# A four-layer graph network on one core: second norm as a factor on ScalarE, edge digits behind the norms, far blocks spread out, count writes issued from ScalarE

## The chip, the cores and the metric

The kernel runs on one core of one Trainium2 chip. The metric is the device time of a whole execution in microseconds (us). The kernel before took 5277.65 us as the median of three runs (5276.34 to 5281.7).

## The reference, cut to what matters

Four layers of a graph network act on 3125 nodes with 256 features and 103,125 edges (50,000 random pairs in both directions, and a loop on every node). Each layer adds a graph attention and a second mixing branch to `x`, and then a feed-forward network. The change touches only what comes first in layer 0:

```python
edge_index = jnp.stack([src, dst])
xn = _layernorm(x, axis=-1)             # (x - mean) / sqrt(var + 1e-5), no weights
x = x + _L0_gnn_ref(xn, edge_index, ...)[...] + _L0_mix_ref(xn[None], ...)[0]
```

`_L0_gnn_ref` is an attention over the edges: each node takes a softmax-weighted sum over its incoming edges. `_L0_mix_ref` takes `xn` as it is for a linear attention over all nodes (a context from keys and values), and it normalizes `xn` a second time, with `ln_g` and `ln_b`, for a gate network (256 to 64, gelu, 64 to 256, sigmoid).

## The kernel before, in words

The nodes lie as 25 tiles of 125 rows (`TP` = 125, `NT` = 25). Work on tiles goes by `GROUPS`: four groups of four tiles, then three of three. The kernel turns the edge list into a dense matrix of counts (how many edges go from source s to destination d), stored in DRAM, and computes graph attention as dense products with these counts.

**Stage A, `begin` (L1592) and `prepare` (L1473).** `run` (L2855) loads x in four pieces (4, 4, 8 and 9 tiles), each by `part_dma` (L571), which issues two DMAs (112 rows and 13 rows), on SP's and ScalarE's queues in turn. `prepare` is a generator. Its first part loads the row table `heads_i` and the destinations, counts by five passes over the table (L1495) where each block of five nodes begins in the sorted edge list, and gathers five edge segments by GpSimd (L1501). `begin` then goes through the groups: `layernorm` (L610: `moments` with L622 and L623, `normed` with a Sqrt on ScalarE L631, a reciprocal L632 and one scaling per tile L634), `transposed` (L286: TensorE transposes L293, one copy to `xT` on ScalarE L301 and one on VectorE L299), and the checks: for every group the matmuls into `p_ends`. For the first four groups it also adds the tiles to the context of keys and values (`context_tile`, L1630: two f32 matmuls per tile with an Exp and a Copy on ScalarE, a memset on GpSimd, two matmuls into `p_ctx`). When `prepare` is sent the fourth group, it first calls `edges()` (L1505): some twenty operations on VectorE that turn the gathered segments into digits (L1509 to L1521), write them to DRAM as `seg_d`, and count the edges found (L1527 to L1545). After the last group the checks are reduced to one number `ok`, on which the kernel branches.

**Stage B, `counts` (L1688).** It reads `seg_d` back, transposes it to digits by edge (L1713, evicted by ScalarE L1715), and goes through 625 groups of five destination nodes in 63 steps of ten groups. In a step VectorE builds two one-hot tiles, `oh_lo` (L1734) and `oh_key` (L1737), from a pool of two buffers. TensorE multiplies them into `p_cnt` (L1750; four PSUM buffers, three used in a step), and ScalarE evicts `p_cnt` as bytes into `stage` (L1752; two buffers). Five steps make a block of 250 destinations. In the five blocks named in `FAR` ScalarE also evicts it as bf16 into `far` (L1755; one buffer). `BLOCKS` gives the order: 8, 0, 9, 1, 10, 2, 11, 3, 12, 4, 5, 6, 7. After a block, SP's queue writes `stage` to `count_d` (L1759, 781 KB) and, for a far block, `far` to `far_d` (L1762, 1562 KB).

Between the steps `counts` advances a second generator, `mix0_pieces` (L1769), at a fixed rate of 93 pieces over 63 steps: `node_pieces` (L1835: projections of the nodes, whose small results go to DRAM by SP's queue, L1856 and L1860), `fold_pieces` (L1651: the other nine tiles of the context), one large addition on GpSimd (L1786), and then by groups the gate network, which begins with `layernorm(xn, xn, group)`, the second norm, in place on VectorE.

**Stage C, `dense_pairs` (L1919).** Its order is written out by hand for all engines. SP's queue loads a row of factors (`q_head`, L1974) and tiles of counts (`a`, L1912; `a_far`, L2019). VectorE multiplies them into `pt` (L1986), and TensorE sums (L2000). For the far destinations ScalarE and GpSimd prepare `pt_far`.

**Order.** Outside of stage C the order of the instructions on each engine and queue is set by the framework's planner. It takes the operations by their place in the program as priority, but moves one ahead of another when its own estimate says that the other isn't ready. Each engine then runs its instructions strictly in that order, DMA issues included: a DMA that can't be issued holds all that stands behind it on the same engine.

Of the kernel before, what the change touches and what calls it, by code (L numbers as in the profile page):

```python
# [10 lines left out]
F32 = mybir.dt.float32  # L11
# [38 lines left out]
NEAR0 = (0, 8)  # L50
FAR0 = (16, 9)
FAR = [8, 9, 10, 11, 12]
BLOCKS = [8, 0, 9, 1, 10, 2, 11, 3, 12, 4, 5, 6, 7]
BEFORE = 4
GROUPS = [(0, 4), (4, 4), (8, 4), (12, 4), (16, 3), (19, 3), (22, 3)]

# [1407 lines left out]
class Dense(Net):  # L1464
# [8 lines left out]
    def prepare(self, pool, xT):  # L1473
# [6 lines left out]
        with ExitStack() as s:  # L1480
# [66 lines left out]

            group = yield
            while group:
                if group == GROUPS[3]:  # L1550
                    found = edges()
                for t in range(group[0], sum(group)):
                    self.mm(p_ends[:, t, :], [(xT[:, k, t * TP:(t + 1) * TP], gw[:, k, C:]) for k in range(KC)])
                group = yield
# [37 lines left out]
    def begin(self, pool, x, xn, xT):  # L1592

        nc, tc = self.nc, self.tc
        self.ctx_d = self.dram.tile([P, KC * (P + 1)], F32, name="ctx_d")
        with ExitStack() as s:
            c = s.enter_context(tc.tile_pool(name="c0", bufs=1))
            w = s.enter_context(tc.tile_pool(name="c0w", bufs=2))  # L1600
            pst = s.enter_context(tc.tile_pool(name="c0t", bufs=2, space=PSUM))
            ps = s.enter_context(tc.tile_pool(name="c0p", bufs=2, space=PSUM))
            ps1 = s.enter_context(tc.tile_pool(name="c0c", bufs=1, space=PSUM))
            wkv = self.keys_weight(c)
            checks = self.prepare(pool, xT)
            next(checks)
            p_ctx = ps1.tile([P, KC, P + 1], F32, name="p_ctx")
            self.context_bank(w, p_ctx, True)
            self.layernorm(xn, x, GROUPS[0])
            for i, (t0, nt) in enumerate(GROUPS):  # L1610
                self.transposed(pst, xT, xn, groups=[GROUPS[i]])
                if i + 1 < len(GROUPS):
                    self.layernorm(xn, x, GROUPS[i + 1])
                checks.send(GROUPS[i])
                if i < BEFORE:
                    for t in range(t0, t0 + nt):
                        self.context_tile(w, ps, p_ctx, xT, wkv, t)
            self.context_bank(w, p_ctx, False)
            part = c.tile([P, KC, P + 1], F32, name="ctx_part")
            nc.scalar.activation(part, p_ctx, AF.Copy)  # L1620
            nc.sync.dma_start(self.ctx_d, part.rearrange("p m f -> p (m f)"))
            next(checks, None)
# [65 lines left out]
    def counts(self, pieces, later):  # L1688


        nc, tc = self.nc, self.tc
        self.count_d = self.dram.tile([NS, P, N], U8, name="count_d")
        self.far_d = self.dram.tile([NS, P, FAR0[1] * TP], BF16, name="far_d")
        B = 10
        with ExitStack() as s:
            c = s.enter_context(tc.tile_pool(name="cnt", bufs=1))
            w = s.enter_context(tc.tile_pool(name="cntw", bufs=2))
            wo = s.enter_context(tc.tile_pool(name="cnto", bufs=1))
            wf = s.enter_context(tc.tile_pool(name="cntf", bufs=1))
            work = pieces(c, wo)  # L1700
            by_edge = []
            ps = s.enter_context(tc.tile_pool(name="cntp", bufs=4, space=PSUM))
            seg = []
            for i in range(2):
                seg.append(w.tile([P, P, 2 * B], BF16, name="oh_lo").rearrange("p a b -> p (a b)").bitcast(F32)[:TP].rearrange("p (g s) -> p g s", s=SEG))
                self.part_dma(nc.scalar if i else nc.sync, seg[i], self.seg_d[i])
            for i, name in enumerate(("lo_t", "key_t")):
                R = 2 if i else 1
                t = c.tile([P, NG, 2, R], BF16, name=name)
                for b in range(GN):  # L1710
                    p = ps.tile([P, 4, KEYS], F32, name="p_cnt")
                    for j in range(2):
                        nc.tensor.transpose(p[:, j, :TP], seg[i][:, b, j * P:(j + 1) * P], self.ident[:TP, :TP])  # L1713
                    for r in range(R):
                        nc.scalar.activation(t[:, b * TP:(b + 1) * TP, :, r], p[:, :2, :TP].rearrange("p i g -> p g i"), AF.Copy)  # L1715
                by_edge.append(t)
            later()
            lo_t, key_t = by_edge
            is_lo = c.tile([P, P, 2 * B], BF16, name="is_lo")
            nc.vector.tensor_copy(is_lo, self.iota[:, :, None].to_broadcast([P, P, 2 * B]))  # L1720
            KP = KEYS + KEYS % 2
            is_key = c.tile([P, KP], BF16, name="is_key")
            nc.vector.tensor_scalar(is_key, self.iota[:, :KP], -127.0, None, op0=OP.add)
            is_pair = is_key.rearrange("p (k r) -> p k r", r=2)
            stage = None
            done, steps = 0, -(-NG // B)
            order = [g0 for k in BLOCKS for g0 in range(k * 50, min(k * 50 + 50, NG), B)]
            for step, g0 in enumerate(order):
                n = min(B, NG - g0)
                m = 2 * n  # L1730
                lo = lo_t[:, g0:g0 + n].rearrange("p g i r -> p (g i r)")
                key = key_t[:, g0:g0 + n].rearrange("p g i r -> p (g i) r")
                oh_lo = w.tile([P, P, 2 * B], BF16, name="oh_lo")
                nc.vector.tensor_tensor(oh_lo[:, :, :m], lo[:, None, :].to_broadcast([P, P, m]), is_lo[:, :, :m], OP.is_equal)  # L1734

                oh_key = w.tile([P, 2 * B, KP], BF16, name="oh_key")
                nc.vector.tensor_tensor(oh_key[:, :m].rearrange("p m (k r) -> p m k r", r=2),  # L1737
                                        key[:, :, None, :].to_broadcast([P, m, KP // 2, 2]),
                                        is_pair[:, None].to_broadcast([P, m, KP // 2, 2]), OP.is_equal)
                at = g0 * GN % 250  # L1740
                if at == 0:
                    stage = w.tile([P, NS, 250], U8, name="stage")
                    far = wf.tile([P, NS, 250], BF16, name="far") if g0 * GN // 250 in FAR else None
                for u in range(0, n, 4):
                    m = min(4, n - u)
                    p = ps.tile([P, 4, KEYS], F32, name="p_cnt")
                    for g in range(m):
                        for i in range(2):
                            j = 2 * (u + g) + i
                            nc.tensor.matmul(p[:, g, :], oh_lo[:, :, j], oh_key[:, j, :KEYS], start=(i == 0), stop=(i == 1))  # L1750
                    o = stage[:, :, at + u * GN:at + (u + m) * GN]
                    nc.scalar.activation(o.rearrange("p t (g d) -> p t g d", d=GN),  # L1752
                                         p[:, :m, :].rearrange("p g (t d) -> p t g d", d=GN), AF.Copy)
                    if far is not None:
                        nc.scalar.activation(far[:, :, at + u * GN:at + (u + m) * GN].rearrange("p t (g d) -> p t g d", d=GN),  # L1755
                                             p[:, :m, :].rearrange("p g (t d) -> p t g d", d=GN), AF.Copy)
                if at + n * GN == 250 or g0 + n == NG:
                    d0, nd = g0 * GN - at, at + n * GN
                    nc.sync.dma_start(self.count_d[:, :, d0:d0 + nd].rearrange("t p d -> p t d"), stage[:, :, :nd])  # L1759
                    if far is not None:  # L1760
                        f0 = FAR.index(d0 // 250) * 250
                        nc.sync.dma_start(self.far_d[:, :, f0:f0 + nd].rearrange("t p d -> p t d"), far[:, :, :nd])  # L1762
                while done < (step + 1) * PIECES0 // steps:
                    next(work, None)
                    done += 1
            for _ in work:
                pass

    def mix0_pieces(self, x, xn, xT, nodes, c, w):  # L1769
# [3 lines left out]
        with ExitStack() as s:  # L1773
# [13 lines left out]
            for t0, nt in GROUPS:  # L1787
                n = nt * TP
                cs = slice(t0 * TP, t0 * TP + n)
                xnn = xn[:, t0:t0 + nt, :]  # L1790
                self.layernorm(xn, xn, (t0, nt))
                yield
                xnnT = w.tile([P, KC, 512], F32, name="xnnT")
                for k in range(KC):
# [1060 lines left out]
    def run(self, x_in, out):  # L2855
# [5 lines left out]
        xn = self.xn_all[:TP]  # L2861
        xT = pool.tile([P, KC, N], F32, name="xT")
        x_v = x_in.rearrange("(t p) c -> p t c", p=TP)
        for i, (t0, nt) in enumerate(((0, 4), (4, 4), (8, 8), (16, 9))):
            self.part_dma(nc.scalar if i % 2 else nc.sync, x[:, t0:t0 + nt, :], x_v[:, t0:t0 + nt, :])
        out_v = out.rearrange("(t p) c -> p t c", p=TP)
        self.begin(pool, x, xn, xT)
# [191 lines left out]
```

## Time and profile before

| what | us |
|---|---|
| median of three runs | 5277.65 |
| profiled execution, its own time | 5526.72 |
| its span, first to last instruction | 5524.8 |
| stage A, to the last write of `ok` | 0 to about 104.6 |
| stage B, from the branch to the last addition to x | 105.4 to 379.2 |
| first VectorE product of stage C | 390.49 |
| last matmul of stage C's end pieces | about 1050 |

Over the whole span TensorE is busy for 4815.9 us, VectorE for 3534.0, ScalarE for 1574.9 and GpSimd for 1522.3. In the first 1035 us TensorE is busy for 918.35 us, VectorE for 854.22, ScalarE for 724.98 and GpSimd for 509.47.

How to read it: a line of the order of time gives the start, the length, the engine, the line of the kernel, the operation with what it writes and reads, how many in a row, and in brackets how long the engine had been idle and what ended that. A letter q after an engine (SPq, ACTq) marks a DMA issue on its queue; its length is the time of the issue, not of the transfer. The profiled execution is longer than the runs without profiling, so that differences in it are compared with its own time.

### The profile page before, as it was taken

The numbers are of one execution on the slowest core, as the hardware profiler recorded it, in microseconds if no ns is written. First come the engines' busy times: TensorE is split into PE (matmuls) and PEld (weight loads), VectorE is DVE, ScalarE is ACT, GpSimd is POOL, SyncE is SP. The second block draws the span as 40 slices with busy tenths as digits, with TensorE's granted clock in tenths as the row PEclk, the third lists the DMA queues.
The fourth block names the chain that finished last, engine by engine and source line by source line (L and its number), as shares of the span: only waits on it lengthen the run. The fifth ranks groups of instructions, "written<-read, shape, count | busy, mean of one in ns | idle before, by whom it ended". The sixth has DMA issues, their size and how long they took to land. (4 is left out here: it accounts for less than half of the span.)

```text
span 5524.8 us, 68126 instructions
## 1 busy us (share of the span) xinstructions
PE 4815.9 (87%) x24840; PEld 2883.0 (52%) x24840; DVE 3534.0 (64%) x5869; ACT 1574.9 (29%) x2503; POOL 1522.3 (28%) x1398
## 2 busy tenths in 40 slices
PE   6889989788888999899998999999967767687768
PEld 4554434477454333686453434556644545454457
DVE  6978888655656998454458997323266666556643
ACT  3668868311421001102330001333311012222221
POOL 1118858244000000000100000000066655555533
PEclk8899999789999999999999999999977888888879
DMA  3875535412100111110001112000154455445535
GB/s 88 89 90 159 160 107 162 134 55 77 49 1 27 34 41 30 43 36 12 14 1 42 39 29 67 14 0 1 37 145 135 137 149 150 135 129 153 143 118 175
DMA packets 353191, 443.06 MB, mean 80 GB/s; under 512 B 144846, under 2 KB 273229, under 8 KB 352278
## 3 DMA queue, kind: packets, MB, share of 16 engines
q1 hardware_dynamic: 264514, 219.66, 16.5%
q0 software_dynamic: 53744, 171.34, 10.8%
q10 hardware_dynamic: 34593, 47.63, 2.8%
q8 instruction: 202, 3.31, 0.2%
q14 instruction: 138, 1.13, 0.1%
HBM read 384.86 MB, written 56.78 MB: 80 GB/s over the span
## 5 line engine op out<-in xcount | busy, mean ns | idle before, releaser
L2289 POOL DMA_INDIRECT z_edge<-tab,src_i x806 | 774.6, 961 | 533.2 <-issue 217.3
L1905 DVE SCALAR_TENSOR_TENSOR pt<-q_head,bar,a 128x750 f32<-128x750 f32 (+2 forms) x800 | 776.3, 1025 | 62.5 <-PE acc L2135 53.8
L2130 PE MATMUL acc<-pt,zs 128*64 128x375 f32 (+2 forms) x3200 | 603.6, 501 | 24.0 <-DVE pt L1905 23.8
L2357 PE MATMUL p_acc<-z_edge,oh 128*125 128x264 f32 x2044 | 555.9, 434 | 41.3 <-DVE z_edge L2348 27.4
L2031 POOL TENSOR_TENSOR pt_far<-pt_far,a_far 128x1125 f32<-128x1125 f32 (+1 forms) x200 | 474.9, 2375 | 280.1 <-DMA a<-count_d 143.6
L2357 PEld LDWEIGHTS p_acc<-z_edge,oh 128*125 128x125 f32 x2044 | 434.4, 217 | 141.8 <-DVE z_edge L2348 29.8
L1986 DVE SCALAR_TENSOR_TENSOR pt<-q_here,bar,a 128x1000 f32<-128x1000 f32 (+1 forms) x384 | 456.1, 1250 | 37.2 <-DMA a<-count_d 15.9
L2130 PEld LDWEIGHTS acc<-pt,zs 128*64 128x64 f32 (+1 forms) x3200 | 247.0, 136 | 357.4 <-issue 221.0
L2000 PE MATMUL p_n<-pt,zs 128*64 128x500 f32 (+1 forms) x1600 | 405.9, 598 | 27.8 <-DVE pt L1986 27.4
L1278 DVE SCALAR_TENSOR_TENSOR x<-p_y,sm,x 125x256 f32<-125x256 f32 x200 | 96.7, 483 | 364.5 <-PE p_y L740 364.5
L2135 PE MATMUL acc<-pt,zs 128*32 128x375 f32 (+2 forms) x3200 | 313.4, 497 | 0.0
L2324 PE MATMUL p_e<-ident,m_sb 128*128 128x128 f32 x202 | 52.9, 352 | 285.1 <-issue 139.6
L2348 DVE TENSOR_TENSOR z_edge<-z_edge,near_e 128x2112 f32<-128x2112 f32 (+1 forms) x101 | 236.6, 2342 | 99.9 <-ACT near_e L2340 75.0
L2185 PE MATMUL acc<-zs,pt 128*125 128x257 f32 x1250 | 275.8, 383 | 11.7 <-DMA a<-count_d 11.7
L2185 PEld LDWEIGHTS acc<-zs,pt 128*125 128x125 f32 x1250 | 234.9, 189 | 52.6 <-issue 14.4
L2000 PEld LDWEIGHTS p_n<-pt,zs 128*64 128x64 f32 (+1 forms) x1600 | 158.9, 137 | 188.7 <-issue 89.9
L2029 ACT ACTIVATE pt_far<-q_log,log_s 128x1125 f32<-128x1125 f32 (+1 forms) x200 | 244.8, 1224 | 31.2 <-PE p_f L2045 28.4
L2045 PE MATMUL p_f<-pt_far,zs 128*64 128x375 f32 (+1 forms) x1200 | 241.9, 483 | 8.1 <-POOL pt_far L2031 8.0
L2030 ACT ACTIVATE pt_far<-pt_far,log_s 128x1125 f32<-128x1125 f32 (+1 forms) x200 | 247.0, 1235 | 6.5
L1262 ACT ACTIVATE h<-p_tr,bn 128x500 f32<-128x500 f32 (+1 forms) x224 | 161.8, 723 | 299.3 <-PE p_tr L740 299.3
L2319 ACT ACTIVATE m_sb<-p_m 128x256 f32<-128x256 f32 x101 | 38.8, 384 | 706.9 <-remote 357.1
L2302 DVE TENSOR_TENSOR hot<-row,near 125x1024 f32<-125x1024 int16 (+1 forms) x149 | 158.5, 1083 | 88.7 <-remote 68.3
(550 smaller groups left out, 7817.7 us busy)
## 6 DMA issues: line engine op xcount, KB each, us to landing
a<-count_d SPq DMA_DIRECT2D x384, 125.0 KB
a_far<-far_d SPq DMA_DIRECT2D x96, 281.2 KB
row<-dst_row SPq DMA_DIRECT2D x101, 224.0 KB
a<-count_d SPq DMA_DIRECT2D x144, 93.8 KB
ef<-in_edge_s SPq DMA_DIRECT2D x101, 128.0 KB
z_edge<-tab,src_i POOLq DMA_INDIRECT x806
count_d<-stage SPq DMA_DIRECT2D x12, 781.2 KB
q_head<-q_g ACTq DMA_DIRECT2D x24, 375.0 KB
```

The source lines that it names most:

```text
L1905: self.nc.vector.scalar_tensor_tensor(pt[:K, :n], q, bar, a[:K, :n], op0=OP.max, op1=OP.mult)
L1986: nc.vector.scalar_tensor_tensor(pt[:K], q[:K], bar[:K, t, h:h + 1], a[:K].rearrange("p (j n) -> p j n", j=2), op0=OP.max, op1=OP.mult)
L2000: nc.tensor.matmul(accs[u][64 * j:64 * j + 64, :M * TP], zs[:K, t, h * W:h * W + 64], pt[:K, j, :], start=(t == 0), stop=(t == NS - 1))
L2029: nc.scalar.activation(f[:K], logs[u, i][:K], AF.Relu, bias=log_s[:K, 0, t, h])
L2030: nc.scalar.activation(f[:K], f[:K], AF.Exp, bias=log_s[:K, 1, t, h], scale=1.0 - 0.2)
L2031: nc.gpsimd.tensor_tensor(f[:K], f[:K], a[:K], OP.mult)
L2045: nc.tensor.matmul(far_accs[u][b][64 * i:64 * i + 64, :n], zs[:K, t, z:z + 64], fs[i][:K, b * n:(b + 1) * n], start=(t == 0), stop=(t == N ...
L2130: nc.tensor.matmul(acc[i // 2][64 * (i % 2):64 * (i % 2) + 64, b, :b1 - b0], zs[:K, t, i * W:i * W + 64], pts[i][:K, b0:b1], **st)
L2135: nc.tensor.matmul(acc[2][32 * i:32 * i + 32, b, :b1 - b0], zs[:K, t, z:z + 32], pts[i][:K, b0:b1], **st)
L2185: nc.tensor.matmul(acc[i], pt[:K, i * TP:(i + 1) * TP], zs[:K, t, :C + 1], start=(t == 0), stop=(t == NS - 1))
L2289: nc.gpsimd.indirect_dma_start(out=zs[i][:, j, :], out_offset=None, in_=table, in_offset=bass.IndirectOffsetOnAxis(ap=src[:, c0 + j:c0 + j ...
L2357: nc.tensor.matmul(acc[t], ohs[i, t][:, k - a, :], zs[i][:, k - c0, :HW], start=(k == cols[t][0]), stop=(k == cols[t][1] - 1))
```

## The change

Five edits are made together.

1. Stage A keeps the variance of each tile (`var`, one small copy per group). After the last group it computes from it, by three operations on VectorE and a Sqrt on ScalarE over 125x25 elements, a factor per node `again`. In stage B the second norm becomes one multiplication by this factor per tile, on ScalarE; since `xn` has mean 0 and variance var / (var + 1e-5), the factor is all that a second norm does.
2. `edges()` is called when the last group is sent, and no longer with the fourth.
3. The order of the blocks is 8, 0, 1, 9, 2, 3, 10, 4, 5, 11, 6, 12, 7.
4. The writes of `count_d` and `far_d` are issued from ScalarE's queue.
5. x is loaded in seven pieces, one per group, in fourteen DMAs.

```diff
-BLOCKS = [8, 0, 9, 1, 10, 2, 11, 3, 12, 4, 5, 6, 7]
+BLOCKS = [8, 0, 1, 9, 2, 3, 10, 4, 5, 11, 6, 12, 7]
...
             while group:
-                if group == GROUPS[3]:
+                if group == GROUPS[-1]:
                     found = edges()
...
-            self.layernorm(xn, x, GROUPS[0])
+            var = w.tile([TP, NT], F32, name="var", bufs=1)
+
+            def norm(t0, nt):
+                mv = self.moments(x, (t0, nt))
+                self.normed(xn, x, (t0, nt), mv)
+                nc.vector.tensor_copy(var[:, t0:t0 + nt], mv[:, :nt, 1])
+
+            norm(*GROUPS[0])
             for i, (t0, nt) in enumerate(GROUPS):
                 self.transposed(pst, xT, xn, groups=[GROUPS[i]])
                 if i + 1 < len(GROUPS):
-                    self.layernorm(xn, x, GROUPS[i + 1])
+                    norm(*GROUPS[i + 1])
+                else:
+                    again = self.again = pool.tile([TP, NT], F32, name="again")
+                    nc.vector.tensor_scalar(again, var, 1.0 + 1e-5, 1e-10, op0=OP.mult, op1=OP.add)
+                    nc.vector.reciprocal(again, again)
+                    nc.vector.scalar_tensor_tensor(again, var, 1e-5, again, op0=OP.add, op1=OP.mult)
+                    nc.scalar.activation(again, again, AF.Sqrt)
                 checks.send(GROUPS[i])
...
-                    nc.sync.dma_start(self.count_d[:, :, d0:d0 + nd].rearrange("t p d -> p t d"), stage[:, :, :nd])
+                    nc.scalar.dma_start(self.count_d[:, :, d0:d0 + nd].rearrange("t p d -> p t d"), stage[:, :, :nd])
                     if far is not None:
                         f0 = FAR.index(d0 // 250) * 250
-                        nc.sync.dma_start(self.far_d[:, :, f0:f0 + nd].rearrange("t p d -> p t d"), far[:, :, :nd])
+                        nc.scalar.dma_start(self.far_d[:, :, f0:f0 + nd].rearrange("t p d -> p t d"), far[:, :, :nd])
...
-                self.layernorm(xn, xn, (t0, nt))
+                for t in range(t0, t0 + nt):
+                    nc.scalar.activation(xn[:, t, :], xn[:, t, :], AF.Copy, scale=self.again[:, t:t + 1])
...
-        for i, (t0, nt) in enumerate(((0, 4), (4, 4), (8, 8), (16, 9))):
+        for i, (t0, nt) in enumerate(GROUPS):
             self.part_dma(nc.scalar if i % 2 else nc.sync, x[:, t0:t0 + nt, :], x_v[:, t0:t0 + nt, :])
```

## The prediction

> **What bounds the kernel now.** I read the page first, then the busy time by stretches of the first 1035 us (the change touches nothing later), then the order of time of each engine around the joints. The early work is three stages, one after the other: A (0 to 105.4 us: load x, norm, transpose, part of the key/value context, checks, ending in the branch on `ok`), B (105.4 to 379: `counts`, with the pieces of the mixing layer between its steps), a gap, and C (from 390.5: `dense_pairs`). Stretches; columns are length, busy time of PE, PEld, DVE, ACT, POOL, then granted clock, DMA share, GB/s:
>
> ```profile
> 62.00:77.20 15.20, 11.17 (x48) 7.72 (x47) 14.86 (x20) 3.02 (x8) 0.46 (x3) 0.79 0.13 42
> 77.20:99.50 22.30, 20.21 (x87) 13.87 (x85) 5.17 (x17) 7.12 (x15) 0.41 (x4) 0.73 0.11 36
> 201.30:226.00 24.70, 15.63 (x134) 12.89 (x134) 17.13 (x16) 16.54 (x42) 4.18 (x3) 0.69 0.77 80
> 226.00:312.00 86.00, 80.29 (x545) 53.02 (x544) 79.78 (x113) 59.64 (x122) 1.03 (x9) 0.97 0.88 80
> 312.00:379.00 67.00, 65.52 (x502) 48.46 (x500) 53.65 (x50) 43.81 (x79) 0.00 (x0) 1.00 0.54 48
> 379.00:390.50 11.50, 0.00 (x0) 0.00 (x0) 0.19 (x2) 0.40 (x1) 0.00 (x0) 0.60 1.28 151
> ```
>
> See: VectorE full at 62 to 77, then TensorE alone at a reduced clock; a hole at 201 to 226 in which no engine is full; TensorE the bound from 226 to 379; then 11.5 us in which only DMA moves. Stage A in order of time:
>
> ```profile
> 51.12 1.82 PE L740 MATMUL p_ends<-gw_g,xT 128*125 128x16 f32 x16
> ...
> 62.34 1.49 DVE L1509 CAST rel<-seg 125x1280 f32<-125x1280 int32 x1 [6.09 <-DMA seg<-in_segments,at_i]
> ...
> 71.53 0.67 DVE L299 COPY xT<-p_tr 128x500 f32<-128x500 f32 x1
> 72.26 3.12 PE L740 MATMUL p_ends<-gw_g,xT 128*125 128x16 f32 x14 [4.03 <-DVE xT L299]
> 76.45 0.17 DVE L632 RECIPROCAL rstd<-rstd 125x3 f32<-125x3 f32 x1
> ```
>
> The edge digits (L1509 to L1533) hold VectorE from 62.3 to 77. The xT copy, whose transposes ended at 66.7, stands behind them until 71.5, TensorE waits 4.03 us for it, and the norm of group 5 (L632) comes only at 76.45. Stage B, the far waits, and SP's queue:
>
> ```profile
> 163.74 1.07 ACT L1755 ACTIVATE far<-p_cnt 128x500 bf16<-128x500 f32 x2 [7.68 <-DMA far_d<-far]
> ...
> 206.14 1.07 ACT L1755 ACTIVATE far<-p_cnt 128x500 bf16<-128x500 f32 x2 [5.67 <-DMA far_d<-far]
> ```
> ```profile
> 153.86 14.77 DVE L1734 TENSOR_TENSOR oh_lo<-lo_t,is_lo 128x2560 bf16<-128x2560 bf16 x1
> ...
> 208.24 1.49 DVE L1734 TENSOR_TENSOR oh_lo<-lo_t,is_lo 128x2560 bf16<-128x2560 bf16 x1 [5.53 <-PE p_cnt L1750]
> ```
> ```profile
> 183.55 4.04 SPq L1762 DMA_DIRECT2D far_d<-far  x1
> 187.69 9.39 SPq L1856 DMA_DIRECT2D q_g<-hg  x1
> ```
>
> ScalarE waits twice for the one far buffer. The first wait lies under a VectorE instruction that took 14.77 us (GpSimd's L1786 ran 153.4 to 167.3); the second reaches VectorE. Issuing a far write takes 4 us, and the next issue on the same queue is held 9.39 us. The joint to C:
>
> ```profile
> 376.77 0.36 SPq L1759 DMA_DIRECT2D count_d<-stage  x1
> 377.22 3.44 SPq L1974 DMA_DIRECT2D q_head<-q_g  x1
> ...
> 390.49 1.26 DVE L1986 SCALAR_TENSOR_TENSOR pt<-q_head,bar,a 128x1000 f32<-128x1000 f32 x1 [11.31 <-DMA a<-count_d]
> ```
>
> **What the Trainium skill says.** (1) "TensorE: Matmul & The Clock Gate", Part 1: an idle TensorE falls to half clock and needs some 3.4 us of work to come back. The trace agrees: 16 p_ends matmuls took 1.82 us at 51, 14 took 3.12 us after the 4.03 us wait. (2) "DMA: Bandwidth & Descriptors", Queues, rings and completion order: SP and ACT each have rings of their own on the same 16 DMA engines, which go round-robin between rings. No row here shows two loaded rings at once. (3) The same page, Issuing engines are not separate DMA queues: a second issuer adds no bandwidth, only issue time. The issue rows above (0.36 to 9.39 us) are that time. (4) "SBUF — State Buffer", two separate sides: VectorE and GpSimd lock each other out of a shared port; it fits the 14.77 us, which the change leaves in place.
>
> **Stage A.** Edge digits go behind the last norm in program order. Removed: the 4.03 us wait; the half clock after it (14 p_ends 3.12 against 1.6, eight context matmuls 3.75 + 2.56 against 3.8: 4 us); and part of the tail 89.6 to 99.5, in which transposes and p_ends of the late groups alternate at about half clock (some 5 us of work in 9.9): 3 to 5. Sum 11 to 13. Added: 7 small copies of var (0.15 each), three ops and a Sqrt for `again`, perhaps a table load (1.28 in the trace): 2 to 3, mostly on engines that wait there. I take a gain of 10. Upper end: at 60.2 TensorE has 23.5 us of full-clock work left (27 x 0.43 context, 28 x 0.11 p_ctx, 52 x 0.11 p_ends, 26 x 0.1 transposes, rest), so it can't end before 83.7 against 99.5: 15.8. Lower end: the order on each engine is a planner's, not the program's (memsets of L1540 ran at 2.5 us), so the digits may stay ahead of the copies: 0, or a loss of 2 with the added ops bare. The digits can't set the end: begun at 62 they end at 77; begun after the last copy at 84 they end near 98, still ahead of 104.4.
>
> The x loads go from 8 to 14 issues in pieces of one group. VectorE waited 12 us in all for x, until 25.7, while DMA was 94% busy up to 18.5 us; but heads_i, which the search L1495 (5 x 3.57 us) needs, stands behind x and moves back. Both sides: a gain of 3, a loss of 2. I take 0.
>
> **Stage B.** *Second norm.* VectorE loses 25 stats (9.4 us), 25 aggregates (3.8), 25 scalings (8.9), reciprocals (1.0): 23 us. But the stats of 17 tiles ran 107.6 to 114.4 while VectorE otherwise waited for the edge transposes until 118.7: worth nothing. About 1 us lies at 178, where VectorE is the bound; some 11 lie at 244 to 312, where TensorE sets the pace and waits for VectorE 4 to 7 us in all. Gain 4, ends 0 and 9. ScalarE gets 25 scalings: 125x256 ACTIVATEs take 0.38 us (0.28 apart) in the trace, a pointer operand adds 0.09 by the page "ScalarE: Activation LUTs" (estimate 25 x 0.37 = 9.3). It loses 7 Sqrt (2.0) and 4 table loads (5.1). Net 2 us on an engine 69% busy: covered, unless they are put before the evictions L1715 that start stage B at 114.7; then up to 9. I take 1.
>
> *Far blocks.* The first wait is under the 14.77 us: 0. The second cost VectorE 5.53 + 1.67. A far write took from 183.55 to 206.1 = 22.6 us; two near blocks of 5 steps at 2.86 us are 28.6, so it is covered. Gain 7 (4 to 7). Between 11 and 12 one near block remains, as before, where no wait showed.
>
> *Issue from ScalarE.* 13 counts x 0.38 and five far writes (4.46, 4.04, 6.69, 3.33, 2.60 = 21.1): 26 us in which ScalarE evicts nothing. Behind it stand the p_cnt evictions, for which TensorE waits, and behind that VectorE's one-hot buffers. Cover: four p_cnt tiles at three per step (3.8 us) and a spare one-hot pair (2.9): 6.7 us, so each of the five alone is hidden or nearly. But other loads are issued on ScalarE's queue at 142.3 and 144.0 (L1786's bias among them), right behind the first far write; held like SP's 10.39 and 9.39, that is about 14 us out less some 3 of work between: 5 over the cover. With 1 for the rest the cost is 6 (0 to 37, below). SP's own holds end; nobody waited there: 0. Stage B: 4 - 1 + 7 - 6 = 4.
>
> **The joint.** q_head (0.5 MB) stood behind the last count write (0.78 MB) and landed 12.9 us after issue, some 100 KB per us. On two rings it lands after twice its own size, 10 us: gain 3 (0 if the write still goes first, 6 if the loads overtake it).
>
> **Sum.** 10 + 4 + 3 = 17 us. The profiled execution takes 5526.72 us (span 5524.8), so 5509.7 by its own time. The median of the runs, 5277.65, is 4.5% below it; most of the 17 us are VectorE and DMA waits and issue time, which I carry over unscaled: **5260.6 us**. About 0.2% (10.6 us) is what a measurement of this kernel can tell from no change.
>
> **Rivals.** *Everything is covered* (0.14): A 15, B 12 (issue hidden, norm 6), joint 5: 32 us, 5245.6. For it: ScalarE is 30% idle. Against: the queue hold is in the trace. *The digits don't move, or their gain is eaten by the next wait* (0.16): A 0, B 4, joint 3: 5270.6. For it: the planner, and p_ctx waits of 2 to 4 us on GpSimd memsets at 58 and 82 that remain. *ScalarE's queue becomes the bound* (0.12): at each of five far blocks issue plus hold is 4.2 + 9.9 = 14.1 us, 7.4 over the cover, 37 in all; the gains without issue cost are 10 + 10 + 3 = 23, so 14 slower: 5291.7. It decides from a hold of 6.7 + 23/5 = 11.3 us per far block. Against it: the next count write on that queue comes a block (14 us) later, when the hold (15.0 us after 139.85, 13.6 after 183.55) is nearly over.
>
> **Numbers.** My forecast has 0.58, with its own range 5251 to 5270. Faster by over 0.2%: nine tenths of it, the first rival and a fifth of the second, 0.69; within: 0.19; slower: 0.12. Range 5243 to 5277: the first three cases with the ends of their costs, without the last.
>
> **What would show it.** Right: no 4 us wait of p_ends for xT, `ok` near 95; no ScalarE wait for far_d; DVE idle near 208 gone; pt of C some 3 us after where the last count leaves. Wrong: edge digits still ahead of xT copies; ACTq rows of 10 us behind far_d with p_cnt waiting on ACT; L1715 later than 9 us after the branch; C still starting 13 us after the last count's issue.

## The result, and the profile after

The kernel after takes 5292.61 us (median of 22 runs, 5265.72 to 5300.71), the kernel before on the same chip 5278.38 us (22 runs, 5252.19 to 5285.05). The ratio is 1.0027 with a 95% interval of 1.0015 to 1.0039: 14 us slower, against 17 us faster foretold. The profiled execution of after took 5296.8 us (span 5294.9), inside the range of its other runs. So profiling is not what made the trace of before long (5526.72 us): e5 below profiles the kernel before on one chip at 5564.3 us, beside 5527 to 5569 of its other runs there. By its granted TensorE clock, 0.922 against 0.940 in the trace of after, that first trace is like those of the slower chips below (0.916 to 0.923); e5 and e6 repeat the comparison on one chip.

The orders of the instructions on TensorE and VectorE are the same in both kernels from stage C on, so that the difference is looked for before it. Four times tell where: `ok` written, the first one-hot tile (start of stage B), the issue of the last count write (its end), and the second product `pt` of stage C. The first product uses one tile of counts; the second waits until the last count write has landed.

| us, first traces | before | after |
|---|---|---|
| `ok` written | 104.4 | 96.3 |
| first one-hot tile | 119.2 | 110.5 |
| last count write issued | 376.8 | 397.5 |
| second `pt` of stage C | 395.2 | 414.1 |

Stage A gains 8.6 us, stage B grows from 257.6 to 287.0 us (+29.4), the joint falls from 18.4 to 16.6 (-1.8): together +19.0 us. Stretches of the kernel after; columns as for the kernel before:

```profile
62.00:77.20 15.20, 12.72 (x48) 8.16 (x47) 13.96 (x16) 3.45 (x10) 0.40 (x4) 0.78 0.19 58
77.20:96.50 19.30, 16.09 (x85) 10.98 (x83) 5.75 (x23) 3.05 (x8) 0.20 (x2) 0.75 0.09 29
110.50:286.00 175.50, 130.61 (x1016) 93.30 (x1015) 139.40 (x133) 106.58 (x261) 17.65 (x13) 0.86 0.60 62
286.00:398.00 112.00, 104.31 (x719) 72.08 (x718) 79.50 (x72) 74.49 (x139) 0.00 (x0) 0.95 0.74 64
```

The tail of stage A is 19.3 us long against 22.3. In the long first part of stage B no engine is full: VectorE, the busiest, works 139.4 of 175.5 us. Most of the time went there. Counted by blocks (block 0 is the first in the order of time, and a block lasts from its first one-hot tile to that of the next), blocks 0 to 6 take 158.2 us against 140.8 before, and blocks 7 to 12, the stretch of the gate network, 128.8 against 116.8. Stage A in order of time:

```profile
61.54 1.49 DVE L1509 CAST rel<-seg 125x1280 f32<-125x1280 int32 x1 [6.55 <-DMA seg<-in_segments,at_i]
...
68.60 0.67 DVE L299 COPY xT<-p_tr 128x500 f32<-128x500 f32 x1
69.32 2.82 PE L740 MATMUL p_ends<-gw_g,xT 128*125 128x16 f32 x14 [2.43 <-DVE xT L299]
71.98 3.75 PE L740 MATMUL p_a<-w_kv,xT 128*125 128x512 f32 x4
```

The digits still stand ahead of one xT copy, but of no norm; the wait is 2.43 us instead of 4.03. The four context matmuls behind it take 3.75 us, as before. Now the two largest holes of stage B, that is, stretches in which the engines stand. The first lies behind the first far write, on ScalarE (line L1772 writes `count_d`, L1775 `far_d`):

```profile
131.72 5.06 ACTq L1775 DMA_DIRECT2D far_d<-far  x1
136.82 0.58 ACT L1869 ACTIVATE hg<-p_a 8x500 f32<-8x500 f32 x1 [5.34 <-issue]
137.04 9.08 ACTq L582 DMA_DIRECT2D v_L_mix_bg<-in_L_mix_bg  x1
...
146.17 0.59 ACT L1765 ACTIVATE stage<-p_cnt 128x500 uint8<-128x500 f32 x1 [6.11 <-issue]
```

ScalarE stands in an issue twice, 5.06 us for the far write and 9.08 us for a load of 1 KB behind it. VectorE is idle for 8.8 of the 13 us from 136 to 149. The second hole follows the second far write, issued at 205.89:

```profile
210.27 1.08 SPq L1874 DMA_DIRECT2D log_g<-gate  x1
222.57 0.80 POOL L1640 DMA_DIRECT2D gate<-in_L_mix_Wqkv  x1 [54.26 <-DMA log_g<-gate]
227.80 3.78 PE L740 MATMUL p_a<-gate,xT 128*125 128x512 f32 x4 [11.33 <-DMA gate<-in_L_mix_Wqkv]
233.70 1.49 DVE L1747 TENSOR_TENSOR oh_lo<-lo_t,is_lo 128x2560 bf16<-128x2560 bf16 x1 [12.86 <-PE p_cnt L1763]
```

To be read downwards: the last small row `log_g` (8 rows of 375 numbers) is issued at 210.27 and lands only at about 222.5. Its staging tile `gate` is also the tile for the context weights, whose load GpSimd can issue only then. The weights land at 227.8. TensorE stands for them for 11.33 us, because the context matmuls are next in its fixed order, and the counting matmuls behind them with it; so VectorE stands for 12.86 us. The joint:

```profile
392.08 0.35 SPq L1988 DMA_DIRECT2D q_head<-q_g  x1
...
401.10 14.23 SPq L1926 DMA_DIRECT2D a<-count_d  x4
```
```profile
401.46 1.26 DVE L2000 SCALAR_TENSOR_TENSOR pt<-q_head,bar,a 128x1000 f32<-128x1000 f32 x1 [1.51 <-DMA a<-count_d]
414.12 1.26 DVE L2000 SCALAR_TENSOR_TENSOR pt<-q_here,bar,a 128x1000 f32<-128x1000 f32 x1 [11.40 <-DMA count_d<-stage]
```

`q_head` is issued 5.5 us ahead of the last count write, no longer behind it, and the first product comes 3.9 us after that write's issue (before: 13.7). The second waits for the write itself.

### The profile page after: what moved, and what is told of

Its sections match the earlier page's. It is cut to its first block, busy times and chain, and to the rows that moved or that the text cites. A ratio compares the mean times of both kernels' runs of the same rounds, so it can differ in the third digit from the quotient of the medians.

```text
span 5294.9 us, 68057 instructions
## 1 busy us (share of the span) xinstructions
PE 4784.9 (90%) x24840; PEld 2853.1 (54%) x24840; DVE 3514.1 (66%) x5797; ACT 1574.6 (30%) x2516; POOL 1525.4 (29%) x1398
## 4 chain that ended last, share of the span: by engine, by line
PE 68%; DVE 12%; issue 6%; POOL 5%; DMA 4%; ACT 3%; ACTq 0%; DVEq 0%; SPq 0%; POOLq 0%; another core or an unknown queue 0%
PE acc L2144 10%; PE p_tr L740 8%; PE acc L2149 5%; PE acc L2199 5%; PE p_acc L2371 5%; PE p_n L2014 5%; PE p_h L740 4%; PE p_y L740 4%; PE p_q L740 4%; PE p_a L740 4%; POOL z_edge L2303 3%; PE p_f L2059 3%; PE p_kvt L740 2%; PE p_o L740 1%; DVE z_edge L2362 1%
## 5 line engine op out<-in xcount | busy, mean ns | idle before, releaser
L2371 PE MATMUL p_acc<-z_edge,oh 128*125 128x264 f32 x2044 | 537.1, 424 | 91.5 <-DVE z_edge L2362 91.5
L2371 PEld LDWEIGHTS p_acc<-z_edge,oh 128*125 128x125 f32 x2044 | 418.3, 208 | 189.6 <-DVE z_edge L2362 100.8
L2199 PEld LDWEIGHTS acc<-zs,pt 128*125 128x125 f32 x1250 | 234.3, 188 | 52.6 <-issue 14.6
L2158 ACT ACTIVATE o<-acc 128x375 f32<-128x375 f32 (+1 forms) x48 | 21.2, 493 | 609.5 <-DMA q_head<-q_g 311.0
L1919 DVE SCALAR_TENSOR_TENSOR pt<-q_all,bar,a 128x500 f32<-128x500 f32 (+3 forms) x175 | 119.0, 682 | 122.2 <-PE acc L2199 118.5
```

The source lines that it names most:

```text
L1919: self.nc.vector.scalar_tensor_tensor(pt[:K, :n], q, bar, a[:K, :n], op0=OP.max, op1=OP.mult)
L2199: nc.tensor.matmul(acc[i], pt[:K, i * TP:(i + 1) * TP], zs[:K, t, :C + 1], start=(t == 0), stop=(t == NS - 1))
L2371: nc.tensor.matmul(acc[t], ohs[i, t][:, k - a, :], zs[i][:, k - c0, :HW], start=(k == cols[t][0]), stop=(k == cols[t][1] - 1))
```

## The experiments

All are whole kernels. They ran in five groups, each on one chip of its own, on which the kernel before took 5551 to 5568 us (groups 1 to 3) or 5288 to 5290 us (4 and 5); so times are given as ratios to the kernel before on the same chip, and traces are compared within a group where it can be. "Stage B" is from the first one-hot tile to the issue of the last count write, "joint" from there to the second `pt`.

| run (group) | first one-hot | stage B | joint | second `pt` | ratio, 95% interval |
|---|---|---|---|---|---|
| e1 loads on SP (1) | 109.1 | 293.4 | 23.2 | 425.8 | 1.0057, 1.0035 to 1.0078 |
| e2 log tile (1) | 109.8 | 285.0 | 23.5 | 418.3 | 1.0015, 1.0000 to 1.0030 |
| e3 writes on SP (1) | 108.8 | 288.2 | 26.4 | 423.4 | 1.0019, 1.0004 to 1.0034 |
| e4 old order (1) | 107.8 | 299.9 | 18.0 | 425.7 | 1.0026, 1.0009 to 1.0043 |
| e5 before (2) | 119.5 | 261.1 | 18.8 | 399.4 | 0.9998, 0.9981 to 1.0016 |
| e6 after (2) | 108.9 | 287.8 | 17.3 | 414.0 | 1.0034, 1.0020 to 1.0049 |
| e7 edit 4 alone (2) | 115.2 | 292.1 | 16.6 | 423.9 | 1.0058, 1.0041 to 1.0075 |
| e8 edit 3 alone (2) | 119.7 | 278.8 | 20.7 | 419.2 | 1.0039, 1.0025 to 1.0054 |
| e9 edits 2, 5 alone (3) | 106.4 | 260.3 | 18.7 | 385.3 | 0.9972, 0.9954 to 0.9991 |
| e10 edit 1 alone (3) | 111.4 | 257.0 | 18.4 | 386.8 | 0.9998, 0.9977 to 1.0020 |
| e11 rows, loads (3) | 111.0 | 269.3 | 15.5 | 395.8 | 0.9982, 0.9963 to 1.0000 |
| e12 combined (3) | 108.1 | 256.3 | 18.3 | 382.7 | 0.9969, 0.9952 to 0.9987 |
| e13 rows alone (4) | 111.9 | 279.5 | 23.5 | 414.8 | 1.0006, 0.9996 to 1.0015 |
| e14 rows, loads, order (4) | 111.9 | 297.5 | 18.5 | 428.0 | 1.0020, 1.0010 to 1.0030 |
| e15 rows, writes on SP (4) | 109.5 | 257.9 | 26.4 | 393.8 | 0.9965, 0.9953 to 0.9977 |
| e16 edits 1, 2, 5 (4) | 107.5 | 270.0 | 21.2 | 398.8 | 0.9978, 0.9964 to 0.9991 |
| e17 rows, old order, SP (5) | 111.3 | 259.9 | 21.0 | 392.2 | 0.9970, 0.9957 to 0.9984 |
| e18 rows, edit 3, SP (5) | 107.9 | 257.1 | 26.2 | 391.2 | 0.9978, 0.9966 to 0.9990 |

**The two holes of the kernel after, one at a time (e1, e2).** e1 moves the small loads away from the far write; `vec` and `row` get an argument `queue`.

```diff
-            g, b = self.vec(c, "L0_mix_ln_g"), self.vec(c, "L0_mix_ln_b")
+            g, b = self.vec(c, "L0_mix_ln_g", queue=nc.sync), self.vec(c, "L0_mix_ln_b", queue=nc.sync)
...
-            bproj = self.row(c, "L0_mix_bproj")
+            bproj = self.row(c, "L0_mix_bproj", queue=nc.sync)
```

> Kernel after, with the five small loads of the mixing layer (v_L_mix_ln_g, ln_b, bg1, bg2, r_L_mix_bproj) issued from SP's queue; the count and far writes stay on ScalarE's. Theory Q (the load behind the first far_d write is held on ScalarE's queue for 9.08 us, and VectorE stands for it): the second block, 24.2 us in the kernel after, takes 15 to 17; the ScalarE holes at 131.7 (5.06, the far issue) stay, the one of 9.08 goes; the last count leaves 7 to 9 us earlier than at 397.5, and the run is some 8 us below the kernel after (about 5285). Rival (the far issue itself and the evictions that pile up behind it are the cost, the load only stands in their shadow): the second block still takes over 21 us and the run stays within 3 us of the kernel after.

The hold of 9 us is gone, and little is gained: blocks 0 to 2 took 72.4 us (30.5, 19.7, 22.2) against 73.1 in e6 (17.2, 24.9, 31.0) and 75.5 in e2, where on the same chip the load is held. The large addition on GpSimd needs `bproj` and so moved from block 2 to block 0, which grew while block 2 shrank. Where the hold was, ScalarE now stands for a small row:

```profile
144.04 5.09 ACTq L1775 DMA_DIRECT2D far_d<-far  x1
...
164.04 0.58 ACT L1869 ACTIVATE hg<-p_a 8x500 f32<-8x500 f32 x1 [5.99 <-DMA q_g<-hg]
```

So theory Q alone fell. e2 frees the weights of the small rows of logs:

```diff
-                e = w.tile([P, KC, 512], F32, name="gate")[:H, 0, :nt * TP]
+                e = w.tile([P, KC, C], F32, name="gwt_g0").rearrange("p k f -> p (k f)")[:H, :nt * TP]
```

> Kernel after, with the small rows of logs staged in the tile gwt_g instead of gate, so that the load of the context weights (gate<-in_L_mix_Wqkv) no longer waits for the last log_g write. Theory W (that write lands 12 us after issue because the far_d write of 1562 KB went ahead of it, the weights land at 227.8, and TensorE stands 11.33 us in its fixed order before the context matmuls): the 11.33 us go, the sixth block takes 22 to 25 us instead of 35.8, the last count leaves 11 to 13 us earlier, and the run is about 5281. Rival (TensorE is short of one-hot tiles or evictions there anyway, and the weights are only the last to come): the sixth block still takes over 31 us and the run gains under 4 us.

TensorE's and VectorE's orders are those of the kernel after, word for word. Block 5 took 24.6 us, as theory W said; the wait for the weights is gone. Beside e1 of the same group (block 5: 38.5) the run is some 0.4% shorter, though e1 has only six runs.

**One part undone (e3, e4).** e3 replaces `nc.scalar` by `nc.sync` in the two writes; e4 restores `BLOCKS`.

> Kernel after, with edit 4 undone (count and far writes issued from SP's queue again). Theory Q: no hold on ScalarE; the second block falls from 24.2 to about 15.5 us and the far issues of 2.7 to 5 us leave ScalarE, 9 to 15 us less in stage B; the joint loses 2 us again; the run 5278 to 5286. Theory W says the sixth block keeps its long wait (over 30 us), since the small writes then stand behind far_d on the same queue as well. Rival (the order of the far blocks, not the queue, cost the 29 us): stage B stays within 4 us of 287.0 us, the run within 3 us of the kernel after.

Block 1 fell to 14.4 us as expected, but stage B stayed at 288.2, the number of the rival: block 5 takes 40.3 (the weights again; VectorE stands for 15.25 us), block 3 21.3, block 11 27.2. With this order and one staging tile, the queue alone is not the cause.

> Kernel after, with edit 3 undone (order of blocks 8, 0, 9, 1, 10, 2, 11, 3, 12, 4, 5, 6, 7 again). Theory F (spreading put two far blocks into the stretch of the gate network, where ScalarE has most work, and one ahead of the last log write): blocks 8 to 12 take some 102 us instead of 112, the wait for the context weights goes, ScalarE waits for far_d again (5 to 8 us, once or twice); stage B is 12 to 18 us shorter than 287.0, the run about 5278. Rival (only the queue of the writes matters): ScalarE's far waits return, nothing else changes, stage B is the same or up to 7 us longer, the run 5292 to 5300.

Wrong on both theories. Stage B is longer, 299.9 us: blocks 3 and 4 take 26.1 and 26.8, with ScalarE standing 8.22 us for `q_g`, and block 5 begins with a wait of 10.1 on VectorE, behind TensorE, which stands for the context weights for 7.86. So the old order doesn't free the weights when the writes are on ScalarE's queue.

**Both kernels and two parts alone, on one chip (e5 to e8).**

> The kernel before, unchanged, for its profile beside the others of this call. Stage B (from the first one-hot tile to the issue of the last count write) 257 us as in the first profile, the ratio to itself 1 within 0.0015 either way: that is what the comparison of times can tell.

Stage B is 261.1 us, 4 more than in the first profile; the ratio is 0.9998, so that the comparison shows nothing where there is nothing.

> The kernel after, unchanged, for its profile beside the others of this call: stage B 285 to 290 us, the run 1.0015 to 1.0039 of the kernel before.

As expected. The second `pt` comes 14.6 us later (stage A -10.6, stage B +26.7, joint -1.5), the run 19 us.

> The kernel before with edit 4 alone (count and far writes from ScalarE's queue). Theory Q (what is behind a far write waits: ScalarE itself for 3 to 6 us of issue, and the small rows of q_g and log_g, whose one staging tile comes free only when the far write has passed): stage B 270 to 285 us against 257, the joint 2 us shorter, the run 8 to 20 us slower. Rival (the order of the far blocks is what costs): stage B 257 to 262, the run within 4 us.

Stage B grew by 31.0 us, the run by 0.58%. Block 1 takes 10.2 us more (load held 9.96), block 3 9.8 more, the rest 0 to 3 each. Block 3 in the trace:

```profile
193.26 3.19 ACTq L1762 DMA_DIRECT2D far_d<-far  x1
...
209.17 1.28 ACT L1855 ACT_TABLE_LOAD   x1 [6.62 <-DMA q_g<-hg]
```
```profile
196.99 0.26 SPq L1856 DMA_DIRECT2D q_g<-hg  x1
```
```profile
212.79 0.17 DVE L1869 COPY es<-p_a 128x8 f32<-128x8 f32 x1 [6.96 <-ACT zs L1868]
```

The row of 12 KB is issued on SP's queue without any hold and still lands 12.2 us later, behind the far write on ScalarE's queue. The Trainium skill ("DMA: Bandwidth & Descriptors", Queues, rings and completion order) has each DMA engine go round between the rings packet by packet; by that a small write on another ring should pass soon. Here it didn't (12.2 us). The row itself isn't slow: in e8 one of 16 KB, issued 22 us behind the last large write, had left its tile after at most 2.7 us, when the tile was written again. Nor does it take a far write: in e6 a row issued 1.0 us behind a count write of 781 KB on ScalarE's queue, 56 us after the last far write, kept ScalarE waiting for its tile until 10.0 us after its issue.

> The kernel before with edit 3 alone (far blocks spread out). The step of the prediction: the second wait for far_d goes, stage B 250 to 254 us. Theory F (two far blocks come into the stretch of the gate network, where ScalarE and TensorE have most work): the wait goes, but blocks 8 to 12 take 105 to 112 us instead of 102, stage B 257 to 267. Theory Q alone says: within 7 us below 257.

The wait for `far_d` goes (block 4: 15.2 us instead of 23.4), and yet stage B is 17.7 us longer. The price isn't in the gate stretch first, as theory F had it (blocks 7 to 11: 107.2 against 101.9), but in block 5 (35.1 against 22.8):

```profile
205.23 3.43 SPq L1762 DMA_DIRECT2D far_d<-far  x1
208.78 10.12 SPq L1856 DMA_DIRECT2D q_g<-hg  x1
219.00 0.29 SPq L1860 DMA_DIRECT2D log_g<-gate  x1
```
```profile
228.29 0.83 POOL L1627 DMA_DIRECT2D gate<-in_L_mix_Wqkv  x1 [8.61 <-DMA log_g<-gate]
```
```profile
237.89 3.78 PE L740 MATMUL p_a<-gate,xT 128*125 128x512 f32 x4 [16.85 <-DMA gate<-in_L_mix_Wqkv]
```

The same chain as in the kernel after, with the writes on SP's queue: the new order puts a far write right ahead of the last pair of small rows.

**The other parts alone, and the theory that is left (e9 to e12).** Theory R: small transfers come through only when a far write has passed, and engines stand for the single tile from which they are sent.

> The kernel before with edits 2 and 5 alone (edge digits behind the norms, x in seven pieces). By the kernel after: ok some 9 us earlier (95 against 105), stage B as before (261 us on this chip), so the first product of stage C and the run some 9 us earlier, 0.9985. Rival (a quicker stage A is given back because the first loads of stage B or the first far write come at another moment): stage B 265 or longer, the ratio within 0.001 of 1.

Better than expected: `ok` at 92.5, stage B 260.3, ratio 0.9972. Neither edit touches stage B, so this is also what stage B takes on this chip.

> The kernel before with edit 1 alone (second norm as a factor by node on ScalarE). The step of the prediction: stage B 4 us shorter (0 to 9), so 252 to 261, ratio 0.998 to 1. Rival (25 more activations on ScalarE delay the evictions): stage B 262 to 270, ratio 1 to 1.002.

Stage B 257.0: 3.2 less than in e9 of the same chip. The ratio, 0.9998, shows nothing of it, nor of `ok`, which came at 97.9: with edit 1 the planner chose another order of TensorE, in which the fourteen p_ends matmuls wait 0.23 us for xT although the digits stay ahead. Why a trace shorter by 12.6 us at the second `pt` left the runs alone stays open; the interval reaches down to 0.9977, 13 us.

e11 is e1's edit, and the rows in four bands of one tile, used in turn:

```diff
-        for t0, nt in GROUPS:
+        if logs:
+            rows = w.tile([P, KC, C], F32, name="gwt_g0").rearrange("p k f -> p (k f)")
+        for i, (t0, nt) in enumerate(GROUPS):
...
-            q = w.tile([64, 512], F32, name="hg")[:H, :nt * TP]
+            r = 64 * (i % 2)
+            q = rows[r:r + H, :nt * TP] if logs else w.tile([64, 512], F32, name="hg")[:H, :nt * TP]
...
-                e = w.tile([P, KC, 512], F32, name="gate")[:H, 0, :nt * TP]
+                e = rows[r + 32:r + 32 + H, :nt * TP]
```

> Kernel after, with the small rows q_g and log_g staged in one tile of four row bands that are used in turn (so that no engine waits for the last pair's writes), and the five small loads on SP's queue. Theory R (what costs is that small transfers come through only when the far write has passed, and that an engine in fixed order stands for their one staging tile or their queue: 9 us in block 1, 13 us in block 5): ScalarE waits for neither q_g<-hg nor a load, the weights come early; stage B 264 to 270 us instead of 287.8; ratio to the kernel before 0.9985 to 1.001. Rival (the far writes' issue on ScalarE and the far blocks in the gate stretch cost most): stage B 278 or more, ratio above 1.002.

As theory R said, which should count the count writes in (see e6 above): stage B 269.3 us, ratio 0.9982, with the order of edit 3 and the writes on ScalarE's queue still in place. VectorE's order is that of the kernel after. The weights are now there long before:

```profile
99.10 0.78 POOL L1640 DMA_DIRECT2D gate<-in_L_mix_Wqkv  x1
```
```profile
197.94 3.59 ACTq L1775 DMA_DIRECT2D far_d<-far  x1
...
211.13 0.41 ACT L1651 ACTIVATE xnnT<-p_a 125x256 f32<-125x256 f32 x1
```

No ScalarE wait for a small write stands between these two, and the context pieces (L1651) run 13 us behind the far write. Blocks 0 to 6 are as short as before (140.5 us, 144.2 in e5). What is not given back lies in the gate stretch: blocks 7 to 11 take 111.7 us against 101.9 in e5.

e12 has edits 1, 2 and 5, the rows in bands, the writes on SP's queue and `BLOCKS = [8, 0, 9, 1, 2, 10, 3, 11, 4, 12, 5, 6, 7]`.

> Edits 1, 2 and 5, the writes on SP's queue, the small rows in four bands, and the order of blocks 8, 0, 9, 1, 2, 10, 3, 11, 4, 12, 5, 6, 7 (far blocks apart, but none behind the middle of the gate stretch). Theory R: the second far wait of 7 us goes, no stall for the weights, stage B 248 to 258 us, ratio 0.9955 to 0.998. Rival (another order of the far blocks brings another stall of its own, as the order of edit 3 did): stage B over 265, ratio above 0.9985.

As expected, 0.9969; but the interval doesn't part it from e9.

**What is left of the loss (e13 to e18).** e13 is e11 without the moved loads, e14 is e11 with the order of e12, e15 the rows in bands with the writes on SP's queue, e16 edits 1, 2 and 5 alone.

> Kernel after with the small rows q_g and log_g in four bands alone; the five loads stay on ScalarE's queue. If the held load is a cost of its own: it is still held for 9 to 10 us behind the first far write, block 1 takes 22 to 26 us, block 5 24 to 26, stage B 274 to 280 us, ratio 0.9995 to 1.002. If the rows were all: stage B within 3 us of 269.3, ratio as with the loads moved (0.998).

The load is held 10.29 us, block 1 takes 26.9, stage B 279.5: the hold is a cost of its own, once the rows don't take its place.

> The kernel of rows in bands and loads on SP's queue, with the order of blocks 8, 0, 9, 1, 2, 10, 3, 11, 4, 12, 5, 6, 7. If far blocks in the gate stretch are what is left of the loss (blocks 7 to 11 took 111.6 us there against 102.0 in the kernel before): those blocks take 101 to 106 us, stage B 257 to 263, ratio 0.995 to 0.9975. Rival (it is the issue and the extra work on ScalarE, wherever the far blocks lie): stage B 266 or more, ratio 0.998 or more.

Wrong: 297.5 us, which is on the side of the rival. One of the holes is again a small transfer behind a far write: the load of the context's first part, 132 KB, issued 9.6 us behind a far write (247.87):

```profile
257.47 0.60 SPq L1678 DMA_DIRECT2D xnnT<-ctx_d  x1
```
```profile
270.39 0.42 DVE L1679 TENSOR_TENSOR xnnT<-xnnT,p_ctx 128x258 f32<-128x258 f32 x1 [9.82 <-DMA xnnT<-ctx_d]
```

The other holes aren't told apart from the issues on ScalarE, 2.66 to 5.62 us each. With this order and the writes on SP's queue e12 took 256.3 us, on another chip.

> Kernel after with the rows in four bands and the count and far writes on SP's queue (edit 4 undone), the order of edit 3. If the far writes' issue on ScalarE (2.7 to 5 us, five times) reaches the end beyond what the evictions' buffers cover: stage B 254 to 263 us, ratio 0.995 to 0.9975. If it is covered, as the prediction took it: stage B within 4 us of 269.3, ratio 0.997 to 0.9995.

Stage B 257.9 us, 21.6 less than e13 of the same chip, ratio 0.9965. The two kernels differ only in the queue of the writes, so the issue and hold on ScalarE aren't covered: 12.2 us of it are block 1, with its held load, and most other blocks give 0.5 to 2.8.

> Edits 1, 2 and 5 without 3 and 4. If the gains add up (stage A 13 us alone, stage B 4 us alone): first one-hot tile at 106 to 109, stage B 255 to 259 us, the steady products of stage C at 380 to 386 against 399, ratio 0.9955 to 0.9975. Rival (the copies of var and the factor cost on the path of stage A what the norm saves in stage B): stage B 255 to 259, but ok no earlier than 95, steady products at 386 to 390, ratio 0.998 or more.

Neither as expected: `ok` at 93.5, but stage B 270.0, with ScalarE standing for `far_d` 11.94, 8.82 and 4.62 us. The far writes were slower on this chip than in group 3: the second was through 25.5 us after its issue, in e9 after 21.7. So whether the gains of edits 1 and 2 add up isn't shown.

> Edits 1, 2 and 5 with the rows in four bands, writes on SP's queue, and the order of blocks of the kernel before. If spreading the far blocks is worth the 7 us that the prediction gave it once nothing small waits behind a far write: the second far wait (5 to 9 us) is here and stage B is 4 to 10 us longer than in e18 of the same call. If the far evictions in the gate stretch eat it: stage B within 3 us of e18 or shorter, the ratios alike within 0.001.

> The same with the order of edit 3 (all of the change but edit 4, and the rows in four bands), beside e17 on one chip: stage B 254 to 262 us, no ScalarE wait for far_d before the last two far blocks, ratio 0.9955 to 0.9985, the lowest of all runs but for the interval.

With the rows in bands the order of edit 3 saves 2.8 us in stage B, no more: block 4 takes 15.1 us instead of 25.4, blocks 10 and 11 together 48.6 instead of 39.4. The wait for `far_d` has moved rather than gone: ScalarE now stands for it in block 11, the last far block, and VectorE behind it for 7.92 us. And the joint takes 5.2 us more, since the last far write is issued only 15.7 us ahead of the last count write:

```profile
337.83 0.59 ACT L1768 ACTIVATE far<-p_cnt 128x500 bf16<-128x500 f32 x1 [7.35 <-DMA far_d<-far]
...
349.33 2.60 SPq L1775 DMA_DIRECT2D far_d<-far  x1
365.02 0.36 SPq L1772 DMA_DIRECT2D count_d<-stage  x1
365.47 9.68 SPq L1991 DMA_DIRECT2D q_head<-q_g  x1
```

In e17 that last issue takes 3.58 us. Spreading the far blocks is worth nothing that the ratios show, 0.9978 against 0.9970, and e18 is not the lowest of all runs.

The kernel of e18 is that of e15, line for line; it gave 0.9965 on one chip and 0.9978 on another. So no version is clearly the best: e9, e12 and e15 to e18, 0.9965 to 0.9978, all lie below both kernels, and none of them sends the writes from ScalarE's queue.

## Why the prediction was wrong

**Stage A (10 us): right in its size, in part by luck.** 8.6 and 10.6 us in two pairs of traces. The mechanism held only in part: a copy still stood behind digits, only 1.6 of the 4.03 us of waiting went, and the four context matmuls behind it were as slow as before (3.75 us). The norms did come ahead of the digits, and the tail is 3 us shorter, as foretold. But e10 shows that the planner can remove the same wait without moving the digits, and in e7 `ok` came 4.0 us earlier than in e5, though edit 4 touches nothing in stage A.

**Second norm (4, less 1): not contradicted.** Stage B is 3.2 us shorter in e10 than in e9. That is one pair of traces; stage B of the kernel before itself took 257.6 and 261.1 us in two. The scalings didn't go ahead of the first evictions, which begin stage B.

**Far blocks (gain 7): this step failed.** The wait for `far_d` went, 8.2 us in block 4 of e8. The step named the near blocks that cover the write, and asked of no other transfer what would stand behind the write at its new place. In e8 that was the last `log_g`, the weights behind it and TensorE behind those: 12.3 us in block 5, and with the rest 17.7 us lost in place of 7 won. Nor is the 7 there once the staging tile is out of the way: e18 wins 10.3 us in block 4 against e17 and loses 9.2 in blocks 10 and 11, where one near block does not cover the write between the last two far blocks, though the step expected no wait there.

**Issue from ScalarE (cost 6, ends 0 and 37): this step failed by its size.** e7 measured 31.0 us. The first hole was named, with its load; 5 us over the cover were 10.2 in block 1. For the rest the prediction allowed 1, on the argument that each issue alone is hidden by four p_cnt tiles and a spare one-hot pair. It left out the rows `q_g`, which no longer stand held on SP's queue but lie written and not landed, with ScalarE in front of their one tile: 9.8 us in block 3. (A row behind a count write alone does the same, 10.0 us from issue to tile in e6, though the prediction charged count writes with their issue only.) "SP's own holds end; nobody waited there: 0" was the sentence that closed this door. Smaller delays of 0 to 3 us per block make the other 11 us.

**The joint (gain 3): near in size for edit 4, by another way.** The step timed the landing of `q_head`. The first product, which needs it, came 9.8 us closer to the last count write, but the second waits for that write itself, and this sets the gain. With the order kept it is 2.2 us shorter in e7, and about 3 in groups 1, 4 and 5 (26.4 to 23.4 with the order of edit 3, 21.1 to 18.2 with the old one). The step overlooked that edit 3 brings a far write to the end: +1.9 us in e8, about 5 in groups 1, 4 and 5.

**The sum.** Stage B was to win 4 us and lost 26.7 in e6; stage A and the joint were near their forecasts. Losses of edits 3 and 4 don't add: 17.7 and 31.0 alone, but 26.7 with all five edits together. The rival that ended on the slow side gave 5291.7, and the measured 5292.61 is close, but by another way. It had issue and hold of 14.1 us at each of the five far blocks; on ScalarE's queue only the first far write had a load close behind it. The second large hole came from a small write on SP's queue. That the number fits is luck; that issue and hold on ScalarE aren't covered, as this rival said, is shown by e13 and e15.

What is shown: edits 3 and 4 each lengthen stage B (e7, e8, on one chip with e5), and removing the staging (e2, e13) and the held load (e11) gives back 18.5 of the 26.7 us, with edits 3 and 4 in place (e11 and e6 on two chips with like holds of far writes). The rest, in the gate stretch, is not taken apart: with one edit alone blocks 7 to 11 take 5.3 us more than in e5 for edit 3 (e8) and 4.6 for edit 4 (e7). That the DMA engines serve the far write's pieces ahead of a small write is inferred from the landing times; no view shows the order within an engine.

## What to carry to other kernels

Before a large transfer is moved in time or to another queue, list the small transfers that will be issued in the next 10 to 20 us on any queue (here one issued 9.6 us behind a far write took 12.9 us), and for each the tile that it holds and the engine that next writes this tile. A staging tile shared by a small write and a later weight load ties the two together; rows in several bands of one tile untied them here at no cost in memory, since a tile was used that is filled only later. And a wait that is removed at one block is worth nothing until the place to which the transfer went has been looked at in the same way.

## What the runs showed of the hardware

A write of 12 KB issued on SP's queue 3.7 us after a far write of 1562 KB on ScalarE's queue landed after 12.2 us (e7), one issued 1.0 us after a count write of 781 KB on that queue after 10.0 us (e6), and one with no large write in the 22 us before it after at most 2.7 us (e8): the other queue was no way past a large write. Where an issue comes right behind one of the first two far writes on the same queue, it is held for 9.1 to 10.1 us in groups 2 and 3 and for 10.2 to 12.7 us in groups 1, 4 and 5. The groups ran on five chips, and the same first row `q_g` on SP's queue was held for 9.3 to 10.1 us in the one set and 11.6 to 12.1 in the other, so that chips seem to differ here by about a fifth; with it differs how much of a far write is covered.
